# Edge sums and maxima of the last six node tiles by one gather of 20 edges per node, instead of by scanned regions

## The chip, the cores and the metric

The kernel runs on one core of a Trainium2 chip. The core has a matrix engine (PE, with its weight loads shown as PEld), a vector engine (DVE), a scalar engine (ACT), a general engine (POOL) that also issues gathers and scatters with computed row numbers, a queue engine (SP) that issues plain transfers, and 16 DMA engines that carry the transfers of all queues. Each engine works through its own list of instructions in order and waits on semaphores for the others. The metric is the time of one execution on the device, in microseconds, as a median of several runs.

## The reference

There are 6250 nodes with 256 features and 100,000 edges with 96 features. The edges come sorted by their destination node `dst`; towards the end of the node list a node has some eight edges. What is computed, cut to the part around the change:

```python
xn   = layernorm(x)
out1 = segment_sum(edge_attr, dst)           # per node: sum of its edges
cnt  = number of edges of the node
out2 = segment_max(edge_attr, dst), 0 where cnt == 0
out3 = out1 / max(cnt, 1)
h    = concat([xn, out1, out2, out3, u[0]])
x1   = x + (relu(h @ W1 + b1) @ W2 + b2) + xn
```

After that every node is normalised again, a gate picks two of 16 experts, each expert is a two-layer network, and the two weighted results are added, normalised and added to `x1`. This second half (the expert stage) is not touched.

## The kernel before, in words

**Tiles and groups.** Nodes are cut into 50 tiles of 125 (`P`), and tiles into 13 groups of up to four (`GS`), taken from the end of the node list to its start (`GRP`). Group 0 holds tiles 46 to 49, and the last group, 12, holds tiles 0 and 1. For a group the kernel normalises `x` (`stats_x`, `root_x`, `scale_x`, `norm_x`), fetches sums and maxima of its nodes (`take_edges`, `take_carry`, `join_edges`, `mask_edges`), transposes all inputs (`turn`), runs the hidden layer on PE (`hidden`, eight steps of five matrix products), the output layer (`output`, four tiles of eight), the residual (`residual`), the second normalisation and the gate (`root_b` to `place`), and scatters the normalised rows to their experts (`send`).

**Edges by regions.** Sums and maxima are not made per node but by running along the edges. The edge list is cut into eight regions (`JR`, from the end of the list): region c has 1000 runs (125 partitions x `RR` = 8) of `JR[c]` edges each. `steps` goes backwards through a run: for each step DVE multiplies the running sum by a flag "the next edge has the same node" and adds the edge, and does the same with min and max (L271 to L275, four operations of 768 elements). Three steps make a chunk (`JS`), which is loaded by `load_edges` (L168) and whose results are stored to `rows_d` (L283), both on SP's queue, with two buffers each. At the end of a region `chain_runs` carries sums across the eight runs of a partition (`over_runs`), across partitions with transposes on PE (`to_features`, `over_partitions`, `to_partitions`), and back (`to_runs`), and stores a carry table (L402). A node's sum is then the row of its first edge plus, where its edges cross runs, one carry row: two gathers of 125 rows per tile on POOL (L593, L600), joined on DVE (L606, L608).

**Where a node's edges begin.** `block_starts` finds the node at the start of each of 400 blocks of 250 edges; `find_block` counts on ACT the blocks that lie before a node (L448), `take_blocks` gathers that block of ids (L457), `find_edge` counts inside it (L464), and `bounds` (L474 to L479) turns this into the first and the last edge of each node. `index_nodes` makes row numbers for the gathers, `counts` the number of edges. This is done in five batches of groups (`IB`). `check_fit` tests that ids are sorted and that the regions suffice for the groups (`GR` says how many groups each region serves); if not, the branch at L1120 works the edges one by one.

**What sets the order.** A list of tasks by slot, written out by hand: a group has 12 slots (`SLOTS`), hidden steps in the first eight, outputs in the other four, and all other steps have a slot before or after. Between slots the edge stream gets what is left of 4.6 us of DVE per slot (`SLOT`, the `credit` in L1192 to L1206), by the costs noted with each step. Where a group asks for its rows, `edges_until` puts all that its region still lacks into the queues at once (L1203). The first region and the start are written out by hand before the branch (L1088 to L1119), the rest of group 0 after it (L1161 to L1188). POOL's queue fetches the weights of the first layer (L1062 to L1068) and of the second (L1071). `fill_rows` (L1056) writes a default to the expert rows at slot 7. When the stream is done, its buffers are given to the expert stage (`open_experts`), which works through 57 blocks of 256 rows; the first 14 of them are made up from the nodes of all groups but the last two, and start beside the end of the last group.

## Time and profile before

| what | value |
|---|---|
| median of three runs | 1474.09 us (1470.38 to 1480.11) |
| the profiled execution's own time | 1469.65 us |
| its span from first to last instruction | 1467.9 us |
| busy PE / DVE / ACT / POOL | 1163.9 / 895.4 / 477.7 / 552.9 us |
| first hidden-layer product (L637) | 90.2 us after the start |
| last edge step of the last region on DVE (L400) | ends near 803.4 us |
| busy PE from 1400 us on | none (the final stage has no matrix products) |
| moved by DMA over the span | 295.11 MB, 201 GB/s |

In the lines of the profile, L12 is line 12 of the kernel. A line of the groups names line, engine, operation, result and sources with their shape (partitions x elements), how often it ran, its total and mean time, and for how long its engine was idle just before it and which instruction or transfer ended that idle time. A line in order of time begins with its start and its duration in microseconds. "x4" stands for four instructions merged. Busy time of PE includes pipelined overlap, so a busy PE is not PE at its peak.

### The profile page before, as it was taken

The page shows a single profiled execution, that of the slowest core. Times are in us where ns is not written, and L with a number is a line of the kernel's source. Part 1 is how long each engine was busy: PE and PEld are TensorE (multiplying, and loading weights), DVE is VectorE, ACT ScalarE, POOL GpSimd, SP SyncE. Part 2 cuts the span into 40 slices and gives each one's busy share as a digit, 9 for nine tenths or more (in the row PEclk, how much of TensorE's full clock was granted, in tenths as well). Part 3 has the DMA queues.
Part 4 walks back from the last instruction along what each step waited for, and adds up shares of the span by engine and source line. Part 5 has one row for each costly group of instructions (what it writes and reads, how often), then busy time and mean ns, then how long its engine had stood idle before and what let it go on. Part 6 is the DMA issues. An engine that isn't in the chain of part 4 may idle for free. (4 is left out here: it accounts for less than half of the span.)

```text
span 1467.9 us, 15866 instructions
## 1 busy us (share of the span) xinstructions
PE 1163.9 (79%) x4588; PEld 818.4 (56%) x4588; DVE 895.4 (61%) x2340; ACT 477.7 (33%) x1034; POOL 552.9 (38%) x623
## 2 busy tenths in 40 slices
PE   0247787978967998989889999898999999999200
PEld 0123535554635556455555667777888888888100
DVE  6557757859758888696975322334445544444397
ACT  2422443425532544524334333231122222122133
POOL 3340633546443366823436411423333333333100
PEclk9988789989988999989899999999999999999655
DMA  7867787878697889977775204555787787765695
GB/s 202 207 154 184 212 247 203 210 185 204 182 235 186 231 232 246 276 205 202 201 217 138 74 6 156 183 197 197 229 263 253 240 262 231 243 227 183 127 263 147
DMA packets 178719, 295.11 MB, mean 201 GB/s; under 512 B 30048, under 2 KB 125633, under 8 KB 171325
## 3 DMA queue, kind: packets, MB, share of 16 engines
q1 hardware_dynamic: 141140, 236.68, 56.9%
q0 software_dynamic: 35984, 55.92, 13.6%
q10 hardware_dynamic: 1497, 1.38, 0.3%
q8 instruction: 39, 0.64, 0.2%
q14 instruction: 59, 0.48, 0.1%
HBM read 167.02 MB, written 128.77 MB: 202 GB/s over the span
## 5 line engine op out<-in xcount | busy, mean ns | idle before, releaser
L639 PE MATMUL pH<-inT,w1a 96*128 96x500 f32 (+1 forms) x624 | 273.7, 575 | 0.0
L946 POOL DMA_INDIRECT y_d<-yb,to_i x114 | 134.7, 1182 | 290.9 <-ACT yb L945 276.9
L927 PE MATMUL pH<-xT,wt 128*128 128x256 f32 x912 | 222.9, 388 | 8.8 <-ACT hb L933 5.1
L753 POOL DMA_INDIRECT xg_d<-xr,pos_i x100 | 127.2, 1272 | 242.5 <-DVE xr L749 139.4
L648 PE MATMUL pO<-w2s,hT 128*125 128x256 f32 x800 | 197.5, 406 | 21.3 <-DVE xt L653 19.7
L940 PE MATMUL pO<-wt,hb 128*128 128x256 f32 x912 | 208.3, 381 | 4.2 <-DVE hb L931 4.2
L639 PEld LDWEIGHTS pH<-inT,w1a 96*128 96x128 f32 x624 | 121.8, 195 | 139.3 <-issue 137.5
L637 PE MATMUL pH<-inT,w1x 128*128 128x500 f32 (+1 forms) x416 | 198.3, 601 | 0.0
L927 PEld LDWEIGHTS pH<-xT,wt 128*128 128x128 f32 x912 | 169.2, 191 | 40.7 <-ACT hb L933 16.0
L940 PEld LDWEIGHTS pO<-wt,hb 128*128 128x128 f32 x912 | 174.2, 191 | 28.9 <-DVE hb L931 5.0
L648 PEld LDWEIGHTS pO<-w2s,hT 128*125 128x125 f32 x800 | 159.1, 203 | 50.2 <-DVE xt L653 22.7
L945 ACT ACTIVATE yb<-yb,xb 128x256 f32<-128x256 f32 x114 | 51.7, 501 | 345.4 <-issue 298.2
L943 DVE TENSOR_TENSOR yb<-pO,xb 128x512 f32<-128x512 f32 x57 | 39.4, 692 | 166.0 <-PE pO L940 166.0
L642 ACT ACTIVATE hT<-pH,c 128x500 f32<-128x500 f32 (+1 forms) x104 | 68.5, 658 | 219.0 <-PE pH L639 218.9
L637 PEld LDWEIGHTS pH<-inT,w1x 128*128 128x128 f32 x416 | 79.2, 203 | 67.8 <-issue 66.9
L457 POOL DMA_INDIRECT gb<-in_dst_dram,blk_i x50 | 69.8, 1395 | 117.8 <-ACT junk L464 34.4
L274 DVE TENSOR_TENSOR rw<-rw,raw 125x768 f32<-125x768 f32 x92 | 89.6, 974 | 29.4 <-DMA raw<-in_edge_dram 29.4
L600 POOL DMA_INDIRECT cg<-carry_d,next_i x50 | 81.8, 1635 | 52.5 <-DMA carry_d<-ct 35.3
L271 DVE TENSOR_TENSOR rw<-rw,keep 125x768 f32<-125x768 f32 x84 | 79.7, 949 | 30.7 <-DMA rows_d<-rw 29.9
L593 POOL DMA_INDIRECT at<-rows_d,first_i x50 | 74.0, 1481 | 39.1 <-issue 27.7
L275 DVE TENSOR_TENSOR rw<-rw,raw 125x768 f32<-125x768 f32 x92 | 87.6, 952 | 0.0
L628 ACT COPY inT<-pT 96x500 f32<-96x500 f32 (+3 forms) x65 | 35.9, 553 | 150.0 <-PE pT L627 149.7
(265 smaller groups left out, 1407.7 us busy)
## 6 DMA issues: line engine op xcount, KB each, us to landing
wt<-in_wpack_dram SPq DMA_DIRECT2D x57, 1026.0 KB
rows_d<-rw SPq DMA_DIRECT2D x26, 1440.0 KB
rows_d<-rw SPq DMA_DIRECT2D x26, 810.0 KB
raw<-in_edge_dram SPq DMA_DIRECT2D x26, 720.0 KB
xb<-xg_d SPq DMA_DIRECT2D x57, 258.0 KB
rows_d<-rw SPq DMA_DIRECT2D x11, 960.0 KB
raw<-in_edge_dram SPq DMA_DIRECT2D x26, 405.0 KB
yk<-y_d SPq DMA_DIRECT2D x20, 400.0 KB
```

What stands on the lines that cost most here:

```text
L271: nc.vector.tensor_tensor(su, prev[0], keep[c][:, :, s + j, None].to_broadcast(bcast), op=OP.mult)
L274: nc.vector.tensor_tensor(su, su, x_j, op=OP.add)
L275: nc.vector.tensor_tensor(mx, mx, x_j, op=OP.max)
L593: nc.gpsimd.indirect_dma_start(out=G[g]["at"][:, i, :], out_offset=None, in_=rows_d[0:PAD + EP * sum(JR[:c + 1]), :], in_offset=IndirectOf ...
L600: nc.gpsimd.indirect_dma_start(out=cg, out_offset=None, in_=carry_d[0:EP * (c + 1), :], in_offset=IndirectOffsetOnAxis(ap=next_i[:, t:t + ...
L637: nc.tensor.matmul(pH[:, :n * P], w1x[:, k, ms], inT[:, k, :n * P], start=(k == 0), stop=False)
L639: nc.tensor.matmul(pH[:, :n * P], w1a[:, k - DC, ms], inT[:EF, k, :n * P], start=False, stop=(k == DC + 2))
L648: nc.tensor.matmul(pO, G[g]["hT"][m][:, i * P:(i + 1) * P], w2s[:, m, :], start=(m == 0), stop=(m == HC - 1))
L753: d = nc.gpsimd.indirect_dma_start(out=xg_d[:, :], out_offset=IndirectOffsetOnAxis(ap=G[g]["pos"][:, i, k:k + 1], axis=0), in_=G[g]["xr"][ ...
L927: nc.tensor.matmul(pB[i][:, half, :], wt[:, k * FF + m * 128:k * FF + (m + 1) * 128], xT[:, k, :], start=(k == 0), stop=(k == DC - 1))
L940: nc.tensor.matmul(pY[:, h, :], hb[:, m, h * 128:(h + 1) * 128], wt[:, W2O + m * D:W2O + (m + 1) * D], start=(m == order[0]), stop=(m == o ...
L946: d = nc.gpsimd.indirect_dma_start(out=y_d[:, :], out_offset=IndirectOffsetOnAxis(ap=BL[b]["to"][:, h:h + 1], axis=0), in_=yb[:, h, :], in ...
```

## The change

The edges of the last six node tiles (44 to 49) no longer pass through regions. For each of their nodes one gather fetches a window of 20 edges (`WE`), 7,680 bytes that end with the node's last edge; a mask built from the node's first edge sets foreign edges to zero for the sum and far down for the maximum; then the 20 edges are summed and maximised. For the two tiles of the first group the masking is split between DVE and ACT and the sum is made on PE by 20 products with the identity; for the four tiles of the second group ACT masks and DVE sums. Both maxima are on DVE.

The first group now holds two tiles (48, 49), and the last group four (0 to 3). Seven regions cover the first 95,000 edges, that is 95 steps in place of 100. The stream of edges starts only at slot 8 of the first group, and the slots of a group of two tiles are given half the time. The padding of `rows_d` goes; a register read by SP places region 0's rows (at the front, or elsewhere if the branch is taken). Weights go from POOL's queue to SP's. The order test gains a test that no node of these tiles has more than 20 edges, and `IB` has six batches, the first two of one group each.

```diff
-JR = (5, 5, 5, 10, 11, 22, 28, 14)
-GR = (1, 1, 1, 2, 2, 3, 2, 1)
+GW = 2
+WE = 20
+JR = (6, 5, 5, 10, 21, 20, 28)
+GR = (1, 1, 1, 2, 3, 2, 1)
...
-IB = (1, 2, 3, 3, 4)
+IB = (1, 1, 1, 2, 3, 5)
...
-    PAD = max(0, N - EP * JR[0])
-
-    REG = [(E - EP * sum(JR[:c + 1]), j) for c, j in enumerate(JR)]
-    GRP = [(max(0, NT - GS * (g + 1)), NT - GS * g) for g in range(NG)]
-    assert N == NT * P and E == EJ * P and EP * sum(JR) == E and NT % FS == 0 and sum(GR) == NG and sum(IB) == NG
+    ER = EP * sum(JR)
+
+    REG = [(ER - EP * sum(JR[:c + 1]), j) for c, j in enumerate(JR)]
+    N0 = NT - GS * (NG - 1)
+    GRP = [(GS * (NG - 1 - g), GS * (NG - 1 - g) + (GS if g else N0)) for g in range(NG)]
...
-        if c == 0:
-            nc.vector.memset(di[:, L:], N)
-            nc.scalar.dma_start(di[0:P - 1], src[0:P - 1])
-            nc.scalar.dma_start(di[P - 1:P, 0:L], src[P - 1:P, 0:L])
-        else:
-            for o, i in halves(di, src):
-                nc.sync.dma_start(o, i)
+        for o, i in halves(di, src):
+            nc.sync.dma_start(o, i)
...
+    def check_order():
+
+        L = L100
+        nc.vector.tensor_tensor(viol[:, 0, :], ids100[:, 0:L], ids100[:, 1:L + 1], op=OP.is_gt)
+        nc.vector.tensor_tensor(viol[:, 1, :], ids100[:, 0:L], ids100[:, WE:L + WE], op=OP.is_equal)
+        nc.vector.scalar_tensor_tensor(viol[:, 1, :], ids100[:, 0:L], float(P * GRP[GW - 1][0]), viol[:, 1, :],
+                                       op0=OP.is_ge, op1=OP.mult)
...
+    def rows_of(c):
+        n, r0 = EP * JR[c], EP * sum(JR[:c])
+        if c:
+            return rows_d[r0:r0 + n, :]
+
+        if not away:
+            away.append(nc.sync.value_load(shift[0:1, 0:1], min_val=0, max_val=n))
+        return rows_d[ds(away[0], n), :]
...
+    def index_windows(g):
+        a, z = GRP[g]
+        n = z - a
+
+        def tmp(name):
+            return ix.tile([P, NT], F32, name=name)[:, 0:n]
+
+        end, at_f, thr = tmp("end"), tmp("f"), tmp("m")
+        nc.vector.tensor_copy(end, ends[g][:, :n])
+        ends[g] = end
+        nc.vector.tensor_scalar(at_f, end, float(-WE), 0.0, op0=OP.add, op1=OP.max)
+        nc.vector.tensor_scalar(win_i[:, a - W0:z - W0], at_f, float(EF), None, op0=OP.mult)
+        nc.vector.tensor_sub(thr, rp[:, a:z], at_f)
+        G[g]["mk"] = mk = ix.tile([P, GS, 2, WE], F32, name="mk", bufs=2)
+        nc.vector.tensor_tensor(mk[:, :n, 0], row_i[:P, None, 0:WE].to_broadcast([P, n, WE]),
+                                thr[:, :, None].to_broadcast([P, n, WE]), op=OP.is_ge)
+        nc.vector.tensor_scalar(mk[:, :n, 1], mk[:, :n, 0], -1.0, BIG, op0=OP.add, op1=OP.mult)
...
+    def take_window(g, i, w):
+        j = GRP[g][0] - W0 + i
+        nc.gpsimd.indirect_dma_start(out=w.rearrange("p k f -> p (k f)"), out_offset=None, in_=flat,
+                                     in_offset=IndirectOffsetOnAxis(ap=win_i[:, j:j + 1], axis=0))
+        G[g].setdefault("win", []).append(w)
+
+    def cut_window(g, i, k0, k1):
+
+        for k in range(k0, k1):
+            w = G[g]["win"][i][:, k, :]
+            nc.scalar.activation(w, w, AF.Copy, scale=G[g]["mk"][:, i, 0, k:k + 1])
+
+    def cut_window_2(g, i, k0, k1):
+        w = G[g]["win"][i][:, k0:k1, :]
+        nc.vector.tensor_tensor(w, w, G[g]["mk"][:, i, 0, k0:k1, None].to_broadcast([P, k1 - k0, EF]), op=OP.mult)
+
+    def sum_window(g, i):
+        nc.vector.tensor_reduce(G[g]["at"][:, i, 0:EF], G[g]["win"][i].rearrange("p k f -> p f k"), AX.X, OP.add)
+
+    def sum_window_2(g, i):
+        G[g].setdefault("pw", []).append(pOp.tile([P, D], F32, name="pO")[:, 0:EF])
+        for k in range(WE):
+            nc.tensor.matmul(G[g]["pw"][i], ident[:P, :P], G[g]["win"][i][:, k, :], start=(k == 0), stop=(k == WE - 1))
+
+    def max_window(g, i):
+        w = G[g]["win"][i]
+        nc.vector.tensor_tensor(w, w, G[g]["mk"][:, i, 1, :, None].to_broadcast([P, WE, EF]), op=OP.add)
+        nc.vector.tensor_reduce(G[g]["at"][:, i, EF:], w.rearrange("p k f -> p f k"), AX.X, OP.max)
+
+    def mask_window(g, i):
+        t, gi = GRP[g][0] + i, G[g]["at"][:, i, :]
+        j = t - W0
+        parts = [(gi, gi, base[0][:, j, :])]
+        if "pw" in G[g]:
+            parts = [(gi[:, 0:EF], G[g]["pw"][i], base[0][:, j, 0:EF]), (gi[:, EF:], gi[:, EF:], base[0][:, j, EF:])]
+        for o, v, b in parts:
+            nc.vector.scalar_tensor_tensor(o, v, nw[:, j:j + 1], b, op0=OP.mult, op1=OP.add)
+        nc.scalar.activation(G[g]["a3"][:, i, :], gi[:, 0:EF], AF.Copy, scale=rc_n[:, t:t + 1])
...
-    region = [c for c, k in enumerate(GR) for _ in range(k)]
+    region = [None] * GW + [c for c, k in enumerate(GR) for _ in range(k)]
...
-                at_slot(B - 9 + i // 2, take_edges, region[g], g, i)
-                at_slot(B - 9 + i // 2, take_carry, region[g], g, i)
+                if g >= GW:
+                    at_slot(B - 9 + i // 2, take_edges, region[g], g, i)
+                    at_slot(B - 9 + i // 2, take_carry, region[g], g, i)
+                else:
+                    for h in range(2):
+                        at_slot(max(0, B - 13 + 2 * i + h), cut_window, g, i, h * WE // 2, (h + 1) * WE // 2)
+                    at_slot(B - 11 + 2 * i, sum_window, g, i, cost=2.2)
+                    at_slot(B - 11 + 2 * i, max_window, g, i, cost=4.4)
+                    at_slot(B - 11 + 2 * i, mask_window, g, i, cost=0.4)
...
-        if n < GS:
-            B += 1
...
+    def loads_1():
+        take_x(0)
+        nc.sync.dma_start(w1x, w1[0:D].rearrange("(k p) h -> p k h", p=128))
+        nc.sync.dma_start(w1a, w1[D:D + 3 * EF].rearrange("(k p) h -> p k h", p=EF))
+        take_x(1)
+        load_ids(0)
+
+    def loads_2():
         nc.gpsimd.dma_start(w1u, w1[D + 3 * EF:D + 3 * EF + GF])
         nc.gpsimd.dma_start(u0, u[0:1].rearrange("a g -> g a"))
         nc.gpsimd.dma_start(b1c, b1.rearrange("(k p) -> p k", p=128))
-        nc.gpsimd.dma_start(b2b, bass.AP(tensor=b2.tensor, offset=b2.offset, ap=[[0, P], [1, D]]))
-
-    def bulk_2():
-        nc.gpsimd.dma_start(w2s, w2.rearrange("(k p) d -> p k d", p=128))
-        nc.gpsimd.dma_start(gws, gate_w.rearrange("(k p) e -> p k e", p=128))
-        nc.gpsimd.dma_start(gbs, bass.AP(tensor=gate_b.tensor, offset=gate_b.offset, ap=[[0, P], [1, NE]]))
-
-    def between_1():
-        index_nodes(0)
-        for i in range(GS):
-            take_edges(0, 0, i)
-
-    def between_2():
-        stats_x(0, 0)
-        stats_x(0, 1)
-        root_x(0)
-
-    between += [between_1, between_2]
-    a, z = node_cols(0)
-    a1, z1 = node_cols(1)
+
+    def loads_3():
+        nc.sync.dma_start(w2s, w2.rearrange("(k p) d -> p k d", p=128))
+        nc.sync.dma_start(b2b, bass.AP(tensor=b2.tensor, offset=b2.offset, ap=[[0, P], [1, D]]))
+        nc.sync.dma_start(gws, gate_w.rearrange("(k p) e -> p k e", p=128))
+        nc.sync.dma_start(gbs, bass.AP(tensor=gate_b.tensor, offset=gate_b.offset, ap=[[0, P], [1, NE]]))
...
-        load_edges(0)
-        load_ids(0)
-        nc.vector.memset(fill, 0.0)
-        if PAD:
-            nc.scalar.dma_start(rows_d[0:PAD].rearrange("(i p) f -> p i f", p=P),
-                                fill[:P, None, 0:2 * EF].to_broadcast([P, PAD // P, 2 * EF]))
-        load_edges(1)
-        take_x(0)
+        loads_1()
+        nc.gpsimd.memset(base[0], 0.0)
+        loads_2()
         more_constants()
         limits()
         nc.scalar.copy(gap, eps_t[0:1])
-        mark_runs(0)
+        nc.vector.memset(fill, 0.0)
         block_starts()
+        check_order()
         for t in reversed(range(a, z)):
             find_block(t)
-        run_edges(3.0)
         take_blocks(a, z)
-        run_edges(3.0)
+        for t in reversed(range(a1, z1)):
+            find_block(t)
         check_fit()
+        take_blocks(z1 - 2, z1)
+        stats_x(0, 0)
         for t in reversed(range(a, z)):
             find_edge(t)
-        for t in reversed(range(a1, z1)):
-            find_block(t)
-        bulk_1()
-        run_edges(7.5)
         bounds(0)
-        take_blocks(z1 - GS, z1)
-        edges_until(0)
+        index_windows(0)
+        for i in range(z - a):
+            take_window(0, i, rawp.tile([P, RR, JS, EF], F32, name="raw").rearrange("p r j f -> p (r j) f")[:, 0:WE])
+        take_blocks(a1, z1 - 2)
+        root_x(0)
         scale_x(0)
         norm_x(0)
...
-        for i in range(GS):
-            take_carry(0, 0, i)
-        load_edges(later.pop())
-        take_x(1)
-        bulk_2()
+        for k in range(DC):
+            turn(0, k)
+        loads_3()
+        for t in reversed(range(a1, z1)):
+            find_edge(t)
+        for i in range(z - a):
+            cut_window_2(0, i, WE // 2, WE)
+            cut_window(0, i, 0, WE // 2)
+            sum_window_2(0, i)
+            if i == 0:
+                bounds(1)
+        index_windows(1)
+        for h in range(2):
+            rw = rwp.tile([P, RR, JS, 2 * EF], F32, name="rw").rearrange("p r j f -> p (r j f)")
+            pair = rw.rearrange("p (h k f) -> p h k f", h=2, f=EF)
+            for i in range(2):
+                take_window(1, 2 * h + i, pair[:, i, 0:WE])
+        for i in range(z - a):
+            max_window(0, i)
+            mask_window(0, i)
         ps_u = eps.tile([128, HC], F32, name="ps")
         for m in range(HC):
-            nc.tensor.matmul(ps_u[:, m:m + 1], G[0]["w1u"][:, m * 128:(m + 1) * 128], u0, start=True, stop=True)
+            nc.tensor.matmul(ps_u[:, m:m + 1], w1u[:, m * 128:(m + 1) * 128], u0, start=True, stop=True)
         nc.vector.tensor_add(c1, ps_u, b1c)
-        for k in range(DC):
+        counts(1)
+        for k in range(DC, DC + 3):
             turn(0, k)
         keep_x(0)
-        run_edges(3.0)
-        for i in range(GS):
-            run_edges(1.5)
-            join_edges(0, i)
-            mask_edges(0, i)
-        for k in range(DC, DC + 3):
-            turn(0, k)
-        for t in reversed(range(z1 - GS, z1)):
-            find_edge(t)
-        take_blocks(a1, z1 - GS)
-        for t in reversed(range(a1, z1 - GS)):
-            find_edge(t)
+        load_edges(0)
+        load_edges(1)
...
-                while credit > 0:
+                while credit > 0 and T >= SLOTS * (GW - 1) - 4:
                     cost_e = next(stream, None)
                     if cost_e is None:
                         break
                     credit -= cost_e
-                T, credit = T + 1, min(credit, 0.0) + SLOT
+                g = min(T // SLOTS, NG - 1)
+                T, credit = T + 1, min(credit, 0.0) + SLOT * (GRP[g][1] - GRP[g][0]) / GS
```

## Prediction

> **What bounds the kernel now.** I read the stages first (busy time of each engine in stretches cut where the work changes), then who waits for whom in the long middle stretch, then single instructions in order of time. In the table of stretches the five pairs are busy us of PE, PE loads, DVE, ACT, POOL; then clock, DMA share, GB/s.
>
> ```profile
> 0.00:68.00 68.00, 10.45 (x37) 7.89 (x37) 39.12 (x136) 19.39 (x47) 22.37 (x31) 1.00 0.81 209
> 68.00:90.00 22.00, 3.10 (x12) 1.96 (x13) 19.41 (x35) 7.97 (x17) 11.39 (x8) 1.00 0.64 179
> 90.00:181.00 91.00, 63.11 (x175) 35.37 (x174) 60.32 (x171) 30.36 (x77) 27.35 (x21) 0.81 0.69 179
> 181.00:803.40 622.40, 539.13 (x1836) 321.13 (x1835) 472.39 (x1244) 251.37 (x525) 303.56 (x272) 0.92 0.80 214
> 803.40:918.00 114.60, 110.54 (x461) 78.17 (x459) 30.62 (x158) 39.82 (x73) 29.44 (x40) 0.97 0.25 76
> ```
>
> At 803.4 the last region's edges are done on DVE. Before that point no engine is full: DVE 591.2 of 803.4 us (39.12 + 19.41 + 60.32 + 472.39), DMA about 0.8. After it PE is 96% busy. The view of waits between 90 and 803 (total, times, longest) tells which of the two sets the pace:
>
> ```profile
> DVE rw L271 <- DMA rows_d<-rw: 29.9, 5, 12.8
> DVE rw L274 <- DMA raw<-in_edge_dram: 29.4, 8, 4.9
> DVE at L606 <- DMA cg<-carry_d,next_i: 26.4, 5, 10.4
> DVE bsa L556 <- DMA xt<-in_x_dram: 16.2, 2, 8.7
> DVE keep L222 <- DMA di<-in_dst_dram: 16.1, 4, 11.8
> DVE rp L474 <- ACT junk L464: 13.8, 1, 13.8
> DVE tmp L398 <- PE ps L392: 8.3, 1, 8.3
> ```
>
> DVE waits for DMA and hardly ever for PE, while PE's waits in the same stretch are for DVE and ACT. So until 803 the clock of the kernel is "DVE work plus DVE waiting for DMA"; then comes a tail that is PE's. In order of time, the start:
>
> ```profile
> 23.71 1.20 DVE L241 TENSOR_REDUCE red<-rw 100x1 f32<-100x1000 f32 x1
> ...
> 68.37 0.22 DVE L486 SCALAR_TENSOR_TENSOR cnt<-cnt,nf,cnt_f 125x4 f32<-125x4 f32 x1 [9.76 <-SPq L1120]
> ...
> 90.20 3.54 PE L637 MATMUL pH<-inT,w1x 128*128 128x500 f32 x4
> ...
> 181.84 1.84 PE L637 MATMUL pH<-inT,w1x 128*128 128x500 f32 x4
> ```
>
> The first hidden layer starts at 90.2, the second group's at 181.8. A group needs about 8 x 4.2 us (L637 with L639) + 4 x 3.6 us (L648) + transposes, some 52 us (the spacing of groups after 803), so group 0 lost about 40 us to stalls.
>
> **What the Trainium skill says.** "VectorE: DVE Perf Modes", the perf-mode tier table: fp32 tensor_tensor and every tensor_reduce run at one element per cycle; its errata section gives (N+151)/0.96 ns. For 768 that is 957 ns, the trace has 952 (L274); for the new 1920 elements it gives an estimated 2.16 us, and L241 (1000 elements, 1.20 us) agrees for a reduce. "SBUF — State Buffer", the port swizzle section: a stride past 16 bytes pays a penalty; no row of before has a DVE read with a 384-byte stride, as the new reduces have. "ScalarE: Activation LUTs", what ACT_TABLE_LOAD costs: 186 ns + 93 per pointer operand + 0.83 per element, successive ones overlapping by 93; for 96 elements and one pointer 359 ns, the trace has 375 (L614), so 0.28 us per new mask step. "DMA: Bandwidth & Descriptors", issuing engines are not separate DMA queues: all queues share 16 engines; its measured table has 1 MB in 6.15 us, but here w2s (1 MB, L1071) took 13.9 us to land beside other traffic.
>
> **The change part by part.**
>
> Start. Edge ids were there before 12.4 (L414); with no edges ahead of them I take 9 (7 to 12). Then L415 to L419 3.1 us, two L448 of 0.76, L452 to L457 0.9: lists issued at 14.5. Gather issues cost 1.4 us each and land after 5 to 9 us (row L457); I take the lists by 22. Two L464 of 0.63, bounds 1.3, the short index 0.6: window gathers issue at 25. Two of 0.96 MB at 209 GB/s are 9 us plus 2: landed at 37. The wait at the branch (9.76) lies beside that. Queued on ACT ahead of the masks are the lists of group 1 (POOL issues two of them behind the windows), 3 us. Masks 10 x 0.28 = 2.8 per tile, 20 PE sums of 0.15 to 0.2 (L627: four in 0.59) = 4 per tile, maxima 2 x 2.16 per tile on DVE, turns 2: first hidden layer near 56 instead of 90.
>
> Group 0 with two tiles keeps PE 26 to 30 us. Meanwhile group 1's windows: ACT 80 x 0.28 = 22, DVE 4 x (3 x 2.16 + 0.4) = 27.5, starting when ACT has masked the first tile (56 + 2.5 + 5.6): DVE is through at 91, group 1's hidden layer starts near 94 instead of 181.8. The residuals of group 0 are queued on DVE behind those reduces; PE does not miss them, for it runs into group 1's turns anyway.
>
> But the edge stream starts there too: 95 steps are left at 91. Before, 95 steps were left at 68. That is the price, and so the sum has to be made on DVE.
>
> DVE work up to the end of the edges. Removed: four of 92 step pairs, each 3.46 (four 768-wide operations, 69.07 to 72.53), 13.8; one chain over a region, 10.3 (0.8 + 3.2 + 1.5 + 4.0 + 0.8 for L347, L357, L379, L398, L222); 12 join operations, 2.8; index passes, 2.5. Added: windows 2 x 6.1 + 27.5 = 39.7; order test 3.3; counts and bounds 1.4. Net +15: 606. Before 91 DVE is busy 17 (tests, constants, index) + 12 + 27.5 + 5 = 62, so idle 29 (it was 31.5 up to 90).
>
> DVE waits after 91. Before they were 713.4 - 532.7 = 181 between 90 and 803. Of these 13.8 go (L474 waited for lists queued behind the weight loads; group 2's lists now are taken during group 0); 12.5 go (L398 for PE 8.3 and L668 4.2 near 790, when PE was behind; it now leads: its sixth tile is done near 161, which is 94 + 52 and a stall of 15, against 208); of the 12.8 at 188 to 201, while fill_rows' 4.2 MB ran (L1056), 4.5 go, because it now runs from about 81, when DVE does not store rows. The carry and store waits I leave. So 150. What is late next is the same stores, loads and carries.
>
> End of edges: 606 + 29 + 150 = 785 instead of 803.4.
>
> Tail. By the costs in the code the stream needs 88 x 3.8 + 7 x 12.7 = 423 and is offered 5 + 10.25 groups x 37.7 (12 slots of 4.6 less 17.5 of tasks) = 391 by slot 135, where group 12 asks for region 6; so it is drained there. Before, the same sum ends it near slot 129, and both have then given DVE the tasks of about 43 tiles. Until then PE holds at the transposes of the chain, so it has left: 4 hidden 16.8, 4 outputs 14.5, turns 8, group 12 of four tiles 33.6 + 14.5, together 88; carry, gather (8 + 5 + 2) lie beside the first 31. With lag I take 100 (92 to 114.6, the old tail). From 918 to the end nothing changes: 550.
>
> Sum: 785 + 100 + 550 = 1435, with the 1.75 us around the span 1436.8 against 1469.65 of the same execution: 33 to 34 us less. The three runs' median is 1474.09, so about **1440**.
>
> Costed at nothing: w1x and w1a go from POOL's queue to SP's, ahead of x of group 1 and the ids of region 0, first needed after 40 and after 91 (SP's issue of such a load took up to 9 us at the start; without that cover the statistics of group 1 would wait). The first two raw loads now wait on SP until DVE is done with the windows that lie in their buffers (near 46 and 50); queued behind them is x of group 2, not issued before slot 7. The zeros of rows_d (0.94 MB, ACT's queue) go. SP's reading of the row offset for region 0 lies in its waits for DVE (L283, 144 us between 181 and 790). The zeroing of base on POOL, 1 to 2 us, ends before POOL has a list to fetch. The last group's steps one slot earlier, and its eight sends instead of four (L753, 1.3 each, +5 us of POOL), lie beside the 14 blocks that don't need them.
>
> Bounds: Weights w2s behind the If share DMA with the windows: 0 to 5 us later. Reduces with stride: 2.16 to 4.3 each, ten of them, 0 to +22; I take 0. Waits 146 to 181.
>
> **Rivals.** (a) *The stage is DMA's.* Up to 803.4 it moved 167 MB at 208 GB/s. The change takes 8.6 MB away (raw 1.9, rows 3.8, zeros 1.0, gathers 1.2, carry 0.8) and adds 5.8. By 91 it has moved about 16.7, and 147.6 remain: at 209 GB/s the edges end at 797, and with the old tail the gain is 7 us: 1467. For it: DMA share 0.80. Against: DVE is 76% busy itself.
> (b) *Late windows.* If a gather of 7,680-byte rows takes not 5 us but 14, as w2s did, group 0 starts at 75 and DVE is through with group 1 at 125: the whole gain is gone. That is the point; at 20 us each (w1a took 23) DVE is through at 155: **1500**, slower. For it: landings of 14 and 23 us in the start. Against: those shared 0.98 of the DMA engines with edge loads.
> (c) *PE's lead carries.* If the waits vanish and PE's lead at the sixth tile (208 - 161 = 47 us) is carried to the tail, with the 15 us of the tail on top: 1412.
> (d) That the fallback branch at L1120 is taken: the inputs have at most 18 edges at a node of the last 750, under 20. No chance.
>
> **Chances.** Forecast 0.60 (own range 1420 to 1459), (a) 0.20, (b) 0.14, (c) 0.06. A run of this kernel can't tell less than about 1% (14.7 us). Faster 0.66, same 0.20, slower 0.14. The range runs to 1415 below, leaving out part of (c), and to 1485 above, leaving out most of (b).
>
> **What would show it.** First hidden layer at 50 to 62 and group 1's at 88 to 100; reduces of 1920 at 2.1 to 2.3 us; the gathers landing within 8 us; last L398 at 770 to 800; from there to the last residual 92 to 110 us; after that 550. Wrong would be: L398's end past 800, or DVE's waits from 91 on above 180 us.

## The result, and the profile after

The changed kernel takes 1537.34 us (median of four runs, 1532.96 to 1541.71), the kernel before 1474.89 us in the same comparison: a ratio of 1.0422, with a 95% interval of 1.0376 to 1.0468. It is 4.2% slower where I had forecast 2.3% faster. The profiled execution took 1532.96 us with a span of 1531.1.

Lines have moved: L224 makes a region's flags, L294 to L298 are the edge steps, L414 the last step of a region's chain, L573 ACT's mean of a window, L546 ACT's masks, L553 and L563 the reduces, L558 the sums on PE, L640 the statistics of x, L690 the joins of carries, L721 the hidden layer. The same table of stretches for the changed kernel (busy us of PE, PE loads, DVE, ACT, POOL; then clock, DMA share, GB/s), cut at the first hidden layer, at group 1's, at the end of the edges and at the last residual:

```profile
0.00:74.50 74.50, 27.71 (x119) 24.84 (x120) 32.34 (x94) 19.94 (x57) 20.50 (x28) 1.00 0.57 137
74.50:148.40 73.90, 35.57 (x134) 28.10 (x134) 43.18 (x41) 39.04 (x128) 10.90 (x8) 0.77 0.34 75
148.40:886.20 737.80, 596.53 (x1997) 353.64 (x1997) 545.91 (x1431) 277.77 (x589) 305.28 (x288) 0.88 0.75 202
886.20:975.30 89.10, 89.04 (x339) 55.73 (x337) 22.62 (x110) 30.30 (x52) 26.82 (x34) 1.00 0.28 87
975.30:1531.00 555.70, 440.07 (x2084) 376.40 (x2084) 274.97 (x607) 130.51 (x299) 159.46 (x254) 0.90 0.69 215
```

The edges end at 886.2 instead of 803.5. In the second row nobody is full: PE works 36 of 74 us, DVE 43, ACT 39, and the DMA engines stand at a third. That is the look of engines that wait for each other in turn. DVE's waits from 91 us, where I expected the edges to begin, to their end:

```profile
DVE at L690 <- DMA cg<-carry_d,next_i: 52.2, 10, 10.0
DVE bsa L640 <- DMA xt<-in_x_dram: 42.2, 5, 11.0
DVE rw L294 <- DMA rows_d<-rw: 17.4, 4, 5.9
DVE blk_f L468 <- ACT junk L464: 17.0, 5, 5.3
DVE at L553 <- ACT rw L546: 16.8, 3, 8.1
DVE rw L297 <- DMA raw<-in_edge_dram: 16.5, 6, 3.9
...
DVE keep L224 <- DMA di<-in_dst_dram: 8.4, 1, 8.4
```

Carries cost 52 instead of 26, x 42 instead of 16, and a wait for ACT's masks is new. Stores and raw loads are down from 59 to 34. In order of time (start and duration, then engine and instruction, in brackets the idle time before it and its releaser), first the start and then one tile of group 1:

```profile
23.09 0.17 DVE L469 TENSOR_SCALAR blk_f<-blk_f 125x2 f32<-125x2 f32 x1 [6.69 <-DVEq L1200]
28.30 0.50 ACT L480 ACTIVATE junk<-gb,nhalf 125x250 bf16<-125x250 int32 x1 [7.16 <-ACTq L1200]
...
45.86 1.16 DVE L550 TENSOR_TENSOR raw<-raw,mk 125x960 f32<-125x960 f32 x1 [10.97 <-DMA raw<-in_edge_dram,win_i]
...
49.23 8.71 PE L558 MATMUL pO<-raw,ident 125*125 125x96 f32 x40 [12.35 <-ACT raw L546]
...
58.49 8.69 PE L558 MATMUL pO<-raw,ident 125*125 125x96 f32 x40
...
74.48 1.88 PE L721 MATMUL pH<-inT,w1x 128*128 128x250 f32 x4
...
100.11 3.51 DVE L553 TENSOR_REDUCE at<-rw 125x96 f32<-125x1920 f32 x1 [6.34 <-ACT rw L546]
103.65 2.16 DVE L562 TENSOR_TENSOR rw<-rw,mk 125x1920 f32<-125x1920 f32 x1
105.84 3.36 DVE L563 TENSOR_REDUCE at<-rw 125x96 f32<-125x1920 f32 x1
109.24 0.42 DVE L572 SCALAR_TENSOR_TENSOR at<-at,nw,xr 125x192 f32<-125x192 f32 x1
109.69 0.38 ACT L573 ACTIVATE a<-at,rc_n 125x96 f32<-125x96 f32 x1 [6.68 <-DVE at L572]
109.98 2.75 ACT L546 ACTIVATE rw<-rw,mk 125x96 f32<-125x96 f32 x10
112.63 0.61 ACT L464 ACTIVATE junk<-b1r,nhalf 125x400 bf16<-125x400 f32 x1
...
113.59 2.75 ACT L546 ACTIVATE rw<-rw,mk 125x96 f32<-125x96 f32 x10
116.24 0.45 ACT L726 ACTIVATE hT<-pH,c 128x250 f32<-128x250 f32 x1
116.37 3.46 DVE L553 TENSOR_REDUCE at<-rw 125x96 f32<-125x1920 f32 x1 [2.43 <-ACT rw L546]
```

Read the last ten lines as a circle. DVE sums, maximises and masks a tile (100.11 to 109.66). Only then can ACT make that tile's mean (L573), for which it has stood idle 6.68 us; and behind the mean in ACT's queue stand the masks of the next tile (L546), for which DVE then stands idle. A tile takes 16.3 us, the length of both engines' work one after the other. The windows of group 1 end at 143.5 us on DVE, its hidden layer starts at 148.4 and the first edge step (L294) at 167.2.

DVE's work and idle time up to the end of the edges, worked out from such stretch tables for every run below (the idle time of a stretch is its length less DVE's busy time):

| kernel | total, us (median) | DVE work | idle to the first hidden layer | idle from there to group 1's | idle from there | edges end |
|---|---|---|---|---|---|---|
| before | 1474.89 | 591.3 | 31.5 | 30.6 | 150.0 | 803.5 |
| changed | 1537.34 | 621.4 | 42.2 | 30.7 | 191.9 | 886.2 |
| late means | 1518.95 | 621.4 | 43.2 | 9.1 | 199.1 | 872.8 |
| folds | 1530.61 | 615.5 | 42.9 | 28.0 | 197.3 | 883.7 |
| sums on PE | 1520.10 | 610.0 | 43.3 | 38.5 | 173.5 | 865.3 |
| no group 1 windows | 1492.80 | 591.6 | 42.5 | 20.5 | 192.1 | 846.8 |
| no planner cost | 1530.83 | 627.4 | 42.5 | 29.7 | 185.5 | 885.0 |
| three together | 1504.68 | 615.1 | 43.8 | 8.7 | 188.6 | 856.3 |
| three, sums on POOL | 1499.78 | 615.9 | 39.7 | 16.5 | 178.2 | 850.4 |
| the same, x earlier | 1485.27 | 614.4 | 41.6 | 14.4 | 161.3 | 831.8 |
| changed, loads moved | 1516.49 | 623.7 | 43.9 | 30.9 | 173.3 | 871.8 |
| before, loads moved | 1458.29 | 588.8 | 34.3 | 32.3 | 136.2 | 791.5 |
| mended | 1478.55 | 622.0 | 43.3 | 2.1 | 163.7 | 831.1 |
| mended, joins later | 1472.38 | 616.9 | 43.8 | 2.1 | 159.3 | 822.0 |

The totals are medians; the other columns belong to one profiled execution of each kernel. That of the changed kernel is its fastest, 4.4 us under its median, so differences of the edges' end come out smaller than those of the medians.

### The profile page after: what moved, and what is told of

Same layout as the page of the kernel before. It is cut to its first block, busy times and chain, and to the rows that moved or that the text cites. A ratio compares the mean times of both kernels' runs of the same rounds, so it can differ in the third digit from the quotient of the medians.

```text
span 1531.1 us, 16029 instructions
## 1 busy us (share of the span) xinstructions
PE 1188.9 (78%) x4667; PEld 838.7 (55%) x4667; DVE 919.0 (60%) x2280; ACT 497.6 (32%) x1124; POOL 523.0 (34%) x611
## 3 DMA queue, kind: packets, MB, share of 16 engines
q0 software_dynamic: 36224, 56.33, 13.2%
## 4 chain that ended last, share of the span: by engine, by line
issue 20%; POOL 10%; PE 8%; DMA 7%; DVE 6%; SPq 2%; POOLq 0%; ACT 0%; DVEq 0%; ACTq 0%
POOL y_d L1030 8%; DMA rows_d<-rw 3%; PE pH L723 3%; PE pO L732 2%; DMA xt<-in_x_dram 2%; PE pH L721 2%; DVE o L1346 1%; DVE o L1345 1%; SPq L1320 1%; DMA yk<-y_d 1%; DMA y_d<-yb,to_i 1%; POOL xg_d L837 1%; DMA raw<-in_edge_dram 1%; DVE bsc L1329 1%; POOL gap L1035 1%
## 5 line engine op out<-in xcount | busy, mean ns | idle before, releaser
L721 PE MATMUL pH<-inT,w1x 128*128 128x500 f32 (+1 forms) x416 | 201.7, 610 | 23.9 <-ACT hT L726 23.9
L837 POOL DMA_INDIRECT xg_d<-xr,pos_i x100 | 121.7, 1217 | 258.0 <-DVE xr L833 176.0
L723 PEld LDWEIGHTS pH<-inT,w1a 96*128 96x128 f32 x624 | 123.0, 197 | 139.5 <-issue 137.3
L1011 PEld LDWEIGHTS pH<-xT,wt 128*128 128x128 f32 x912 | 170.2, 192 | 40.5 <-ACT hb L1017 15.4
L1027 DVE TENSOR_TENSOR yb<-pO,xb 128x512 f32<-128x512 f32 x57 | 39.4, 692 | 165.0 <-PE pO L1024 165.0
L721 PEld LDWEIGHTS pH<-inT,w1x 128*128 128x128 f32 x416 | 79.7, 205 | 91.9 <-issue 65.1
L297 DVE TENSOR_TENSOR rw<-rw,raw 125x768 f32<-125x768 f32 x88 | 85.1, 967 | 16.5 <-DMA raw<-in_edge_dram 16.5
L294 DVE TENSOR_TENSOR rw<-rw,keep 125x768 f32<-125x768 f32 x81 | 78.9, 974 | 19.0 <-DMA rows_d<-rw 17.4
L298 DVE TENSOR_TENSOR rw<-rw,raw 125x768 f32<-125x768 f32 x88 | 83.6, 950 | 0.0
L684 POOL DMA_INDIRECT cg<-carry_d,next_i x44 | 67.9, 1543 | 45.7 <-DMA carry_d<-ct 31.8
L991 DVE COPY xT<-pT 128x512 f32<-128x512 f32 x57 | 39.4, 691 | 72.1 <-PE pT L989 69.7
L295 DVE TENSOR_TENSOR rw<-rw,bar 125x768 f32<-125x768 f32 x81 | 77.0, 950 | 0.0
```

What stands on the lines that cost most here:

```text
L294: nc.vector.tensor_tensor(su, prev[0], keep[c][:, :, s + j, None].to_broadcast(bcast), op=OP.mult)
L295: nc.vector.tensor_tensor(mx, prev[1], bar[c][:, :, s + j, None].to_broadcast(bcast), op=OP.min)
L297: nc.vector.tensor_tensor(su, su, x_j, op=OP.add)
L298: nc.vector.tensor_tensor(mx, mx, x_j, op=OP.max)
L721: nc.tensor.matmul(pH[:, :n * P], w1x[:, k, ms], inT[:, k, :n * P], start=(k == 0), stop=False)
L723: nc.tensor.matmul(pH[:, :n * P], w1a[:, k - DC, ms], inT[:EF, k, :n * P], start=False, stop=(k == DC + 2))
```

## The experiments

All kernels are variants of the changed one unless said otherwise. The theory to start with: *the order of ACT's queue* (the circle above) delays the edges, and the delay passes through to the end. Rivals: the strided reduces; something later than the start.

### ACT's means after all masks

```diff
-        nc.scalar.activation(G[g]["a3"][:, i, :], gi[:, 0:EF], AF.Copy, scale=rc_n[:, t:t + 1])
+        if g == 0:
+            mean_window(g, i)
...
+                    at_slot(B - 4, mean_window, g, i)
```

> ACT makes the four means of group 1 (L573) only in slot 8, after all its masks; nothing else is changed. Theory of the order (ACT's means wait for DVE and hold up the next tile's masks, which DVE waits for): DVE's 24 us of waiting for masks shrink to under 10, the windows of group 1 end at 118 to 126 us on DVE instead of 143, its hidden layer starts near 125 instead of 148, the first edge step near 145 instead of 167, and the whole is 15 to 24 us shorter than the changed kernel (1513 to 1522 us). Rival, the strided reduces set the pace: DVE has the same work, so no more than 5 us are gained.

Measured: 1518.95 us, ratio to before 1.0288 (1.0234 to 1.0342), 18.4 us less than the changed kernel. DVE in order of time:

```profile
85.69 3.45 DVE L553 TENSOR_REDUCE at<-rw 125x96 f32<-125x1920 f32 x1 [8.26 <-ACT rw L546]
...
94.86 0.42 DVE L572 SCALAR_TENSOR_TENSOR at<-at,nw,xr 125x192 f32<-125x192 f32 x1
95.55 3.42 DVE L553 TENSOR_REDUCE at<-rw 125x96 f32<-125x1920 f32 x1
...
124.23 0.42 DVE L572 SCALAR_TENSOR_TENSOR at<-at,nw,xr 125x192 f32<-125x192 f32 x1
```

One wait of 8.3 us is left, at the first tile; then a tile takes 9.8 us without a gap, the windows end at 124.7, and group 1's hidden layer starts at 127.7. The circle is shown: the means cost 21.6 us of DVE's idle time, of which 13.4 arrive at the end of the edges; the two profiled executions are 12.9 us apart (1532.96 and 1520.11). DVE's work is the same, so the strided reduces don't explain this part.

### Folds in place of strided reduces

```diff
-        nc.vector.tensor_reduce(G[g]["at"][:, i, EF:], w.rearrange("p k f -> p f k"), AX.X, OP.max)
+        fold(G[g]["at"][:, i, EF:], w, w, OP.max)
...
+    def fold(o, w, d, op):
+        nc.vector.tensor_tensor(d[:, 0:8], w[:, 0:8], w[:, 8:16], op=op)
+        nc.vector.tensor_tensor(d[:, 0:4], d[:, 0:4], w[:, 16:20], op=op)
+        nc.vector.tensor_tensor(d[:, 0:4], d[:, 0:4], d[:, 4:8], op=op)
+        nc.vector.tensor_tensor(d[:, 0:2], d[:, 0:2], d[:, 2:4], op=op)
+        nc.vector.tensor_tensor(o, d[:, 0], d[:, 1], op=op)
```

> Sums and maxima of the windows by five additions or maxima of halves over contiguous rows (1920 to 768, 384, 384, 192, 96) instead of one reduce with a stride of 384 bytes; arithmetic the same up to the order of the sum. Five such operations cost 2.5 to 2.9 us by the rows of 768 (0.95), 192 (0.42) and 96 elements (0.30), the reduce 3.4. Theory of the order: each tile's link in the chain gets 1.2 to 1.6 us shorter, the start of the edges comes 6 to 8 us earlier, the whole is 5 to 8 us shorter (1529 to 1532). Rival, the strided reduces are what is lost: the whole gets at least 12 us shorter.

Measured: 1530.61 us (1.0358, 1.0306 to 1.0411), 6.7 us less, nearer to the theory of the order than to the 12 of the rival; but the intervals of the two kernels overlap, so the medians alone don't decide. The profiles do better: a fold costs 2.7 us (0.96 + 0.56 + 0.56 + 0.36 + 0.26), a reduce 3.4, DVE's work falls by 5.9, and the edges end 2.5 us earlier. The strided reduces are a small part of the loss.

### Group 1's sums on PE

```diff
-                    at_slot(B - 11 + 2 * i, sum_window, g, i, cost=2.2)
+                    at_slot(B - 11 + 2 * i, sum_window_2, g, i)
```

> Group 1's sums are made on PE by 20 products with the identity (8.7 us a tile, as group 0's), DVE keeps the maxima: 13.7 us less DVE work. Theory of the order: a tile's turn is masks 5.5, sum 8.7 on PE behind the hidden steps queued there, then the maximum 5.5 which overwrites what PE reads, so 20 us or more instead of 16.2; the windows end later, and the whole is 5 to 30 us longer than the changed kernel. Rival, DVE's work sets the pace before the edges start: the whole is 8 to 14 us shorter.

Measured: 1520.10 us (1.0302, 1.0252 to 1.0353), 17.2 us less. My expectation was wrong by sign, and the gain is larger than the rival's 8 to 14. One tile, from PE's and DVE's order of time:

```profile
91.70 0.31 DVE L572 SCALAR_TENSOR_TENSOR at<-at,nw,xr 125x96 f32<-125x96 f32 x1
92.51 8.71 PE L558 MATMUL pO<-rw,ident 125*125 125x96 f32 x40 [2.35 <-ACT rw L546]
101.26 2.16 DVE L562 TENSOR_TENSOR rw<-rw,mk 125x1920 f32<-125x1920 f32 x1 [8.88 <-PE pO L558]
```

I had set masks (5.5 us) and the sum on PE (8.7 us) one after the other. But each product needs one masked edge only: PE starts at 92.51, right after the first mask, and runs beside the rest. A tile takes 15.4 us on average instead of 16.7 (from the first to the fourth: 46.2 and 50.1 us for three), DVE waits more in this stretch (38.5 against 30.7) and yet has 11.4 us less work; and the waits for x in the edge stage are 23.5 instead of 42.2. By the table the edges end 20.9 us earlier: 11.4 by less work and 18.4 by less idle time in the edge stage, against 8.9 more idle time before it. So most of this gain lies in waits that the run wasn't made to change. The edges began 19 us earlier, which made me suspect the planner's costs, tried two headings below.

### No windows for group 1

```diff
-                take_window(1, 2 * h + i, pair[:, i, 0:WE])
+        nc.gpsimd.memset(G[1]["at"], 0.0)
...
-                    at_slot(B - 11 + 2 * i, sum_window, g, i, cost=2.2)
-                    at_slot(B - 11 + 2 * i, max_window, g, i, cost=4.4)
+                    at_slot(B - 11 + 2 * i, lambda g, i: None, g, i, cost=6.6)
```

> Left out: the gathers, masks, sums and maxima of group 1's four tiles; their sums and maxima are zero. The planner's costs stay. Theory of the order: only group 0's work and the planner's slots are left before the edges; group 1's hidden layer starts at 105 to 112 instead of 148, the first edge step at 120 to 130 instead of 167, and 37 to 50 us come off the whole (1487 to 1500): the loss at the start passes through to the end one to one. Rival, the edges are held by something later (gathers and loads after 170, PE behind): less than 25 us come off the whole though the edges start 40 us earlier.

Measured: 1492.80 us (1.0114, 1.0058 to 1.0169), 44.5 us less, with the first edge step at 123.0, 44 us earlier. The start of the edges passes through to the end one to one here. But the run takes away more than a delay: of the 39.4 us by which the edges end earlier, 29.8 are DVE work that is no longer done and 10 are idle time, so it does not show that a mere delay passes through. It is a bound: with group 1's windows at no cost at all the kernel is still 1.1% slower than before. So a second loss sits elsewhere; the table shows it in the last column of idle time, 192 us as in the changed kernel, where the kernel before has 150.

### No planner cost for the windows

```diff
-                    at_slot(B - 11 + 2 * i, sum_window, g, i, cost=2.2)
-                    at_slot(B - 11 + 2 * i, max_window, g, i, cost=4.4)
-                    at_slot(B - 11 + 2 * i, mask_window, g, i, cost=0.4)
+                    at_slot(B - 11 + 2 * i, sum_window, g, i)
+                    at_slot(B - 11 + 2 * i, max_window, g, i)
+                    at_slot(B - 11 + 2 * i, mask_window, g, i)
```

> Only numbers of the planner are changed: the windows of group 1 (sums, maxima, masks in slots 1 to 7) cost it nothing, so that it places the first edge steps at slot 8 and not after five more slots of small steps. Theory of the planner (in the run with sums on PE the windows ended 5 us earlier, but the edges began 19 us earlier, because its sums had no cost): the windows still end at 143, the first edge step starts at 145 to 152 instead of 167, and 13 to 20 us come off the whole (1517 to 1524). Rival, the sums on PE gained by taking work from DVE: here that work is still there, so at most 5 us come off.

Measured: 1530.83 us (1.0369, 1.0321 to 1.0417; its interval overlaps that of the changed kernel). The first edge step comes at 145.1, as foreseen, and the edges end at 885.0 instead of 886.2. The planner's theory falls: steps moved ahead of small tasks, and those tasks, it seems, only came later with their waits (no line here follows them). The time of the first edge step is no measure of progress; DVE's work and waits are.

### The three together

Late means, folds and no planner cost.

> Late means, folds instead of strided reduces, and windows without cost for the planner, together. By the parts: a tile's windows take DVE 8 us, four of them from 84 on end near 116 to 120, the first edge step starts at 118 to 126, and the whole takes 1537 less the 41 to 49 us by which the edges start earlier: 1488 to 1497. If the edge stage gets longer as it starts earlier, 1500 and more.

Measured: 1504.68 us (1.0200, 1.0155 to 1.0245). The windows end at 119.7 and the first edge step is at 120.3, but the edge stage is 17 us longer, the second case of the expectation. By the table it is made up of DVE's work 6.3 us less, idle time in the windows 22.0 less and after them 3.3 less, before them 1.6 more.

### Sums on POOL, and x three slots earlier

```diff
+                index_windows(1)
...
+                sum_window_2(0, i)
+            else:
+                sum_window(0, i)
...
+        fold(G[g]["at"][:, i, 0:EF], G[g]["win"][i], chp.tile([P, RR, EF], F32, name="tmp"), OP.add, nc.gpsimd)
```

> As the three together, and besides: group 1's index and gathers go out ahead of the PE sums of group 0, its first tile is masked ahead of the slots, the sums of group 1 and of group 0's second tile are folded on POOL (4.5 to 5.5 us each by its 2.61 us for 1024 elements, L670), beside the maxima on DVE. Expected: first hidden layer near 70, windows of group 1 done at 98 to 108, first edge step at 102 to 112, whole 1470 to 1486. If POOL's additions or their wait on each maximum (it overwrites what the sum reads) take longer, windows end after 115 and nothing is gained over the three together.

Measured: 1499.78 us (1.0180, 1.0124 to 1.0236), and windows that end after 115: the second case. DVE and POOL in order of time, each operation once alone and once beside the other engine:

```profile
74.24 1.00 POOL L558 TENSOR_TENSOR tmp<-tmp 125x384 f32<-125x384 f32 x1
79.64 0.96 DVE L556 TENSOR_TENSOR rw<-rw 125x768 f32<-125x768 f32 x1
...
86.59 2.97 POOL L558 TENSOR_TENSOR tmp<-tmp 125x384 f32<-125x384 f32 x1
88.74 1.63 DVE L556 TENSOR_TENSOR rw<-rw 125x768 f32<-125x768 f32 x1
...
111.96 2.16 DVE L569 TENSOR_TENSOR rw<-rw,mk 125x1920 f32<-125x1920 f32 x1 [9.03 <-POOL tmp L557]
```

The interval overlaps that of the three together, so nothing is shown to be gained. The two engines hold each other up (a POOL addition took 2.97 us instead of 1.00, DVE's 1.63 instead of 0.96), and the last tile's sum stood in POOL's queue behind four gathers of id lists. The next kernel only moves the loads of x:

```diff
-                at_slot(B - 17, take_x, g)
+                at_slot(B - 20, take_x, g)
```

> As the run before it, and the loads of x are put into SP's queue three slots earlier (group's slot less 20 instead of less 17). DVE waited 42 us for them after 166. If those waits are time of the edge stage, 15 to 40 us come off; rival, what is late next takes their place (rows stored, raw loads, carries): less than 8 us, with the waits of DVE for carries or rows up by what those for x lose.

Measured: 1485.27 us (1.0080, 1.0045 to 1.0114), 14.5 us less. DVE's waits for x fall from 35.7 to nothing that the view lists, those for stored rows rise from 20.3 to 34.9, and idle time from group 1's hidden layer on falls by 17. So x is a true cost of the stage, though part of it comes back as another wait. Why x is late shows in the changed kernel, in SP's and DVE's order of time:

```profile
587.14 1.60 SPq L305 DMA_DIRECT2D rows_d<-rw  x2
588.85 4.59 SPq L172 DMA_DIRECT2D raw<-in_edge_dram  x2
593.54 3.11 SPq L630 DMA_DIRECT2D xt<-in_x_dram  x1
...
610.77 0.43 DVE L640 BATCH_NORM_STATS2 bsa<-xt 125x6 f32<-125x256 f32 x1 [8.56 <-DMA xt<-in_x_dram]
```

The load of x is queued just behind a chunk's stores and loads and lands 14 us after its issue (596.6 to 610.8); three slots are not enough. In the kernel before this happened to two groups, in the changed one to five.

### The loads moved in both kernels, and a mended version

The same two moves in the changed kernel and in the kernel before: x as above, and the ids of the next region at the start of a region.

```diff
-                c2, s2, n2 = chunks[i + 2]
-                if c2 and s2 + n2 == JR[c2]:
-                    load_ids(c2)
...
                 mark_runs(c)
+                if c + 1 < len(JR):
+                    load_ids(c + 1)
```

> The changed kernel with only its loads moved: x three slots earlier in SP's queue, and the edge ids of the next region at the start of a region instead of two chunks before they are needed. The windows stay as they are. Theory (the second half of the loss is DVE's waits in the edge stage, 42 us for x where I had left the 16 of before, and 8 to 19 for ids): DVE's idle time from group 1's hidden layer to the last edge falls from 192 to 155 to 170, and 20 to 35 us come off (1502 to 1517). Rival, carries and stores take their place: less than 10 us.

> The same two moves of loads in the kernel before (x three slots earlier, ids of the next region at the start of a region). If these waits belong to the edge stage of either kernel, before gains what it waits there, 16 for x and 16 for ids less what comes in their place: 1445 to 1465 us, and the changed kernel with the same loads stays some 45 to 60 us behind it. If they are something that the change brought, before does not get faster by more than 6 us.

Measured: the changed kernel 1516.49 us (1.0282, 1.0234 to 1.0331), 20.8 less; the kernel before 1458.29 us (0.9887, 0.9837 to 0.9936), 16.6 less. So these waits belong to the edge stage of either kernel and not to the change; the distance between the two is 58 us, where it was 62. The idle time of the changed kernel fell to 173.3, less far than expected, as rows (17 to 30) took part of it. The kernel before with these two moves is the fastest of all, 1.1% faster than the kernel before as it was.

The mended version joins late means, folds, no planner cost, index and gathers of group 1 ahead of the PE sums, its first tile masked ahead of the slots, and both moves of loads.

> Of the changed kernel: late means, folds, no cost for the planner, index and gathers of group 1 ahead of the PE sums, its first tile masked ahead of the slots (all sums of group 1 on DVE, none on POOL), and the two moves of loads. By the parts: windows done at 108 to 113, DVE idle in the edge stage about 165, edges done near 822 to 832, the whole 1464 to 1477: the same as the kernel before, or up to 10 us faster.

Measured: 1478.55 us, 1.0031 (1.0012 to 1.0050) of before, 1.5 us above the range that was expected. Its stretches up to the last residual:

```profile
0.00:74.30 74.30, 27.71 (x119) 24.85 (x120) 30.98 (x102) 25.36 (x77) 19.81 (x28) 1.00 0.68 160
74.30:118.00 43.70, 29.66 (x134) 24.05 (x134) 41.63 (x74) 34.88 (x110) 12.39 (x8) 0.95 0.36 86
118.00:831.10 713.10, 593.82 (x1997) 352.75 (x1997) 549.38 (x1431) 276.44 (x587) 323.24 (x288) 0.90 0.78 209
831.10:920.10 89.00, 88.98 (x338) 55.72 (x336) 22.62 (x108) 30.31 (x52) 26.84 (x34) 1.00 0.28 87
```

DVE is idle 2.1 us in the second row. Its whole idle time (209.1) is now that of the kernel before (212.2), and its work is 30.7 us more; the tail is 25.8 us shorter and the rest of the program 5.5 longer. That adds up to the 7.3 us between the two spans, 1475.2 and 1467.9: with no more idle time than the kernel before, the change loses to more DVE work before the edges' end what the shorter tail gives. By DVE's busy time in the whole span (895.4 and 918.9) 23.5 of the 30.7 us are new; the rest stood behind the edges before. And the mended version has the two moves of loads, which have nothing to do with the change. Against the kernel before with the same moves (1458.29 us) it is 20 us slower, 1.4% (with later joins, below, 14 us): even mended, the windows cost more than they save.

The last run joins carries one slot later:

```diff
-                at_slot(B - 6 + i // 2, join_edges, g, i, cost=0.6)
-                at_slot(B - 5 + i // 2, mask_edges, g, i)
+                at_slot(B - 5 + i // 2, join_edges, g, i, cost=0.6)
+                at_slot(B - 4 + i // 2, mask_edges, g, i)
```

> As the mended version, and the joins of carries and the masks of groups 2 to 12 one slot later (joins from the group's slot less 5, masks from less 4; PE's transposes of them stay at less 3). DVE waits 63 us for carries there, in long waits of 8.8 to 16.4 us just after a region's end. Theory (these waits are time of the edge stage, since edge steps could run in them): they fall below 45, and 10 to 20 us come off the mended version (1459 to 1469). Rival, PE's transposes or stores and raw loads wait instead: less than 5 us come off.

Measured: 1472.38 us, 1.0011 (0.9989 to 1.0033) of before; 6 us less than the mended version, between the 10 to 20 of the theory and the rival's less than 5; the intervals overlap, so whether anything was gained isn't settled. (The 63 us that the expectation names count carries up to 870 us; the lines below end with the edges.) DVE's waits in the edge stage, first mended, then with later joins:

```profile
DVE at L701 <- DMA cg<-carry_d,next_i: 49.5, 10, 16.4
DVE rw L296 <- DMA rows_d<-rw: 29.9, 5, 9.1
...
DVE rw L299 <- DMA raw<-in_edge_dram: 12.9, 6, 4.9
```

```profile
DVE rw L296 <- DMA rows_d<-rw: 42.6, 7, 11.9
DVE rw L299 <- DMA raw<-in_edge_dram: 22.7, 9, 5.0
DVE rw L296 <- DMA raw<-in_edge_dram: 18.3, 2, 10.4
...
DVE at L701 <- DMA cg<-carry_d,next_i: 16.6, 5, 8.2
```

The carries gave back 33 us and stores and raw loads took most of it. That could speak for the prediction's rival (a), transfers as the limit beneath all of these versions. Against it: in its edge stage (from 182 us) the kernel before with moved loads carried 219 GB/s at a DMA share of 0.82, the last version 212 at 0.78, the changed kernel 202 at 0.75, so the later versions did not carry the most that this stage has carried. No run took transfers away, and the question stays open.

## Why the prediction was wrong, step by step

| term of the sum | predicted | measured |
|---|---|---|
| DVE work to the end of the edges | 606 | 621.4 |
| DVE idle up to group 1's hidden layer | 29 | 72.9 |
| DVE idle from there to the end of the edges | 150 | 191.9 |
| end of the edges | 785 | 886.2 |
| tail to the last residual | 100 | 89.1 |
| the rest of the span | 550 | 555.8 |
| around the span | 1.75 | 1.86 |
| profiled execution | 1436.8 | 1533.0 |

The form of the sum held: each run's end is DVE's work plus its idle time plus a tail. Two of its terms failed, by some 44 and 42 us.

**"Group 1's windows: ACT 22, DVE 27.5 ... DVE is through at 91" (failed).** I laid ACT's and DVE's work side by side and asked only for the first masks. Where the mean (L573) stands in ACT's queue, behind DVE's work on one tile and ahead of the masks of the next, I had not written down. DVE was through at 143.5. The run with late means brings 19 us of this back in the windows' end, and 18.4 in the whole by the medians.

**"First hidden layer near 56" (failed, 74.5).** Lists went out at 13.2 and 14.8, about where I had said (14.5). Then ACT stood 7.16 us and DVE 6.69 at the branch (L1200), which I had let lie beside other work: the second list was counted at 28.3, and the window gathers went out at 31.3 and 32.8 instead of 25. The first mask started at 45.9, 14.6 us after the first issue, where I had 12 (25 to 37). The PE sums took 8.7 us a tile instead of 4: an fp32 product of 96 columns with 125 rows stands as two records, on average 0.218 us apart (8.71 / 40), where I had taken the time of transposes, one record each. Group 1's bounds were queued on PE behind the first tile's sum, so that its index waited 8.3 us. These are read from the trace, and their shares of the 18 us aren't settled: with the bounds ahead of the sums (mended) the wait of 8.3 fell to 1.1 and the first hidden layer still started at 74.3, and with one of the two PE sums gone (sums on POOL) at 73.2.

**"Waits after 91 = 150" (failed).** I took three waits away (13.8, 12.5, 4.5) and left the others as they were. The lists' wait only changed place (L468 and L490, 17.0 from 91 on and 6.3 before), the wait for PE in the chain (8.3) did go, and carries and x rose by 52 us between them while stores and raw loads fell by 25. I had carried waits over as if they were a property of the code. For x they depended on which chunk's transfers stood ahead of its load in SP's queue, and the runs with x earlier settle that. Why the carries wait 52 instead of 26 stays open. In the kernel before, too, they rose, from 26 to 39, when its loads were moved and its total fell.

**DVE work (+15).** The added operations were counted well. Ten strided reduces took 3.36 to 3.51 us instead of 2.16, together 12.5. The bound of 4.3 that I named held them, but I took the lower end. DVE also does 22.6 us in the tail where it did 30.8 before, so 8 us of tasks stand earlier. Together that is 20.5; what takes 5 of it back I did not trace.

**Tail (right in direction).** 89.1 instead of 114.8, just under the 92 that I gave as its lower bound. **The rest (550)** is 5.8 longer. The eight scatters of the last group, which I had costed at nothing, end at 982; that they cause it is argued, not shown.

**The rivals.** (b) named the right stage, the start, and the right sign: DVE through with group 1 past 125 and the gain is gone. Its mechanism was not what happened: the two gathers of group 0 let the first mask start 14.6 us after the first issue, 2.6 more than in the forecast, where (b) had each of them take 14 or 20 instead of 5. That its first hidden layer at 75 came out (74.5) is luck; the branch, the PE sums and the queue order made up the rest. (a) can't be told apart from the forecast in the changed kernel, where transfers had become fewer per time (DMA share 0.75 in the stage, 0.80 before), and the mended versions leave it open.

## What to carry to other kernels

When two in-order engines hand a tile back and forth, write down both queues in program order before calling their work parallel: one late instruction (here a 0.4 us mean) placed ahead of the next tile's first step makes the sum of both out of the longer of the two. Waits for transfers are not constants of a stage; after a shift they fall on other loads, so keep the range as wide as the whole sum of such waits. And ask of a change what work it adds to the engine that sets the stage: this one added DVE work before the edges' end (591.3 to 621.4 us) and could win only by a shorter tail and by less idle time, and the shorter tail alone (25.7 us) did not pay for it.

## What the runs showed of the hardware

- A reduce over 20 elements at a stride of 384 bytes (1920 elements, fp32, 96 results) took 3.36 to 3.51 us, an operation over the same 1920 in order 2.16 and a reduce of 2000 in order to one result 2.23 (L251): a factor of about 1.6 where the Trainium skill ("SBUF — State Buffer", port swizzle section) only speaks of a penalty. That the stride costs it, and not the 96 short reduces in one instruction, no run separates.
- The Trainium skill ("SBUF — State Buffer", the section on two separate sides) says that a DVE operation with two inputs in SBUF and a POOL operation that reads it exclude each other for a whole instruction. The traces agree that such operations hold each other up: beside each other, 2.97 us for 1.00 on POOL and 1.63 for 0.96 on DVE; in the run with x earlier a DVE operation of four elements a partition, 0.15 us elsewhere, took 1.70 beside a POOL addition of 2.01.
- Passing the branch (L1200) cost DVE 6.69 and ACT 7.16 us, idle time that the profile puts down to the branch itself and to no other engine or transfer; why it takes so long isn't shown.
